# Two chained normalised 5x5 convolutions: outer output rows copied straight from PSUM, part of a row transform moved from VectorE to ScalarE and adding transfers, reflections on GpSimd, one buffer for statistics pieces

## The chip, the cores and the metric

The kernel runs on one core of one Trainium2 chip. A core has TensorE (PE, matrix products into PSUM), VectorE (DVE), ScalarE (ACT), GpSimd (POOL), SyncE (SP, which here only sends transfers) and 16 DMA engines that all queues share. The metric is device time in microseconds, lower is better. Before the change the median of three runs is 1880.79 us (1878.82 to 1884.2).

## The reference

The input x is 8 images of 32 channels, 252 x 252, float32. Two layers of the same form follow one another:

```python
def conv(x, weight):                       # 5x5, reflected edges, by FFT
    p = weight.shape[-1] // 2
    xp = jnp.pad(x, ((0, 0), (0, 0), (p, p), (p, p)), mode='reflect')
    wp = jnp.roll(zeros_like_xp.at[:, :, :5, :5].set(weight), shift=(-5 // 2, -5 // 2), axis=(-2, -1))
    out = ifft2(einsum('bihw,oihw->bohw', fft2(xp), fft2(wp))).real
    return out[:, :, p:-p, p:-p]

def _gn(v, G=16, eps=1e-5): ...            # group norm over 2 channels and all pixels

x = x + conv(_gn(x), L0_conv_weight)
x = x + conv(_gn(x), L1_conv_weight)
return x
```

So per image and layer: mean and variance of 16 groups, a 5x5 convolution of 32 to 32 channels on the normalised image, and the image itself added.

## The kernel before

**Layout.** The four pixel phases (even or odd row, even or odd column) times 32 channels lie on the 128 partitions (`quad`), so the 5x5 convolution becomes a 3x3 one of 128 to 128 channels on a quarter of the pixels. The normalisation's scale and the residual are folded into the weights of each image, and its mean goes in as a bias of one product.

**Chunks.** An image's layer is 8 chunks of 16 phase rows (`NCH`, `ROWS`), and `order` lists all chunks of all images and layers: while layer 1 of image b + 1 runs, its chunks alternate with those of layer 2 of image b. A "pair" below is a chunk of layer 2 and the layer-1 chunk beside it, some 27 us. In the code layers count from 0, so `l == 1` is layer 2. Layer 1's output stays on the chip in tiles `y`, one for a chunk, which are layer 2's input.

**Row transform.** In each group of four rows six combinations of input rows ("points" 0 to 5) are made, each is convolved along the columns with its own weights, and the six results are combined into four output rows. `transform` makes the points. It builds v (sums or differences of rows two apart) and u (two combinations, 4 times one row plus or minus the row two below), and from them `t`: point 2 (L592) is a difference of u's two halves, point 1 (L602) their sum, points 4, 3 and 0/5 (L596, L599, L609) come from v. For most chunks of layer 2 (`sent`) v is made by GpSimd's transfers: a copy of `y` into v (L557), and, once it has landed, two adding transfers (L559, L560), the second for the last two rows, which come from the next chunk's `y`. u is made by VectorE (L576, L577, and L584 for the last row). v has one buffer (tag `va`) through most of the run, so the next copy waits for L609, the last reader.

**Products.** `conv` runs on TensorE: points 2 and 4 into the banks `m`, 1 and 3 into `pairs`, on top of m's values that ScalarE puts there as a start (`seed`, L729 and L731), then 0 and 5 into `sums`. For part of the chunks (`by_columns`) points 0 and 5 use a column transform of their own (`columns`, L618 to L628, `column_product` at L707, `column_parts`), which has fewer products and more VectorE work. VectorE combines the results: L748 for differences, `inner` (L757, L758) writes output rows 1 and 2 of each group into `y`, `parts05` and `column_parts` add what rows 0 and 3 need into `sums`. ScalarE then copies rows 0 and 3 from `sums` into `y` (`outer_columns` L785, `outer` L773).

**Statistics of layer 1's input.** Each image is read a second time in 14 pieces (`load_piece` L254, tile `st`, two buffers in `spool`), and ScalarE sums each piece and its squares (L235, L241) an image ahead. `keep` does the squares for layer 2's statistics (L860) and reflects the edges of `y` by four narrow copies on ScalarE (L869 to L872).

**Output.** `store` puts layer 2's rows, of which the two column phases lie on different partitions, side by side into a tile `o` (four pairs of ScalarE copies per chunk, L925) and SP sends them out (`send_rows` L910). For the last chunk but one (`end`) VectorE and GpSimd do this.

**Order.** The order of instructions on each engine is written out by hand: `at(t, fn)` enters a step with a planned time, the table is sorted by it, and each engine runs its instructions in that order. The planned times set the order only; what is waited for follows from the data. `begin(i)` is the planned start of the i-th chunk.

Of the kernel before, what the change touches and what calls it, by code (L numbers as in the profile page):

```python
# [45 lines left out]
ALU = mybir.AluOpType  # L46
# [10 lines left out]
def tile_conv_preact_x2(ctx: ExitStack, tc: tile.TileContext, x: bass.AP, w0: bass.AP, w1: bass.AP, out: bass.AP):  # L57
# [18 lines left out]
    spool = ctx.enter_context(tc.tile_pool(name="spool", bufs=2))  # L76
# [168 lines left out]
    def load_piece(b: int, i: int):  # L245
        src = x[b].rearrange("ch h w -> (ch h w)").rearrange("(p n) -> p n", p=P)
        if b == 0:
            t = ypool.tile([P, PIECE], F32, tag="y", name=f"st_{b}_{i}")
        else:
            t = spool.tile([P, PIECE], F32, tag="st", name=f"st_{b}_{i}")  # L250
        parts = 3 if (b, i) == (0, NPIECE - 1) else 1
        m = PIECE // parts
        for j in range(parts):
            S.dma_start(t[:, j * m : (j + 1) * m], src[:, i * PIECE + j * m : i * PIECE + (j + 1) * m])  # L254
        pieces[b, i] = t
# [281 lines left out]
    def transform(t0: float, t1: float, b: int, l: int, c: int, free: float = -100.0, now=(0, 0, 0)):  # L537
# [3 lines left out]
        sent = l == 1 and (b, c) != (0, 0)  # L541

# [6 lines left out]
        def row_sums(add: bool):  # L549

            t, nxt = source()
            if not add:

                i = max(order.index((b, l, c)) - order.index((B - 2, 1, NCH - 2)), 0)
                got["v"] = vpool.tile([P, ROWS, wi], F32, tag=("va", "v")[i % 2], name=f"v_{b}_{l}_{c}")
                got["vt"] = got["v"].rearrange("p (t i) w -> p t i w", i=4)
                G.dma_start(got["v"], t)  # L557
            else:
                G.dma_start(got["v"][:, 0 : ROWS - 2], t[:, 2:ROWS], accum_op=ALU.add)  # L559
                G.dma_start(got["v"][:, ROWS - 2 : ROWS], nxt[:, 0:2], accum_op=ALU.add)  # L560

# [50 lines left out]
        def columns():  # L612
# [7 lines left out]
            if m == mo:  # L620
                f = "p t e (m a) -> p (t e) a m"
                V.tensor_sub(
                    d.rearrange("p t e a m -> p (t e) a m"),
                    t[:, :, :, 0 : 2 * m].rearrange(f, a=2), t[:, :, :, 2 : 2 * m + 2].rearrange(f, a=2),
                )
            else:
                V.tensor_sub(d[:, :, :, 0], t[:, :, :, 0 : 2 * m : 2], t[:, :, :, 2 : 2 * m + 1 : 2])
                V.tensor_sub(d[:, :, :, 1, 0:mo], odd[:, :, :, 0:mo], t[:, :, :, 3 : 2 * mo + 2 : 2])  # L628
# [15 lines left out]
        else:  # L644
            if sent:
                two = begin(order.index((b, l, c)) - 2)
                at(two + 1.45, row_sums, False)
                at(two + 8.4, row_sums, True)
            else:
                at(t0, row_pairs)  # L650
            for dt, fn in ((2, row_quads), (3.2, last_rows), (3.6, point2)):
                at(t0 + dt, fn)
# [8 lines left out]
    def conv(b: int, l: int, c: int, t0: float, t1: float, t2: float = 0.0, j0: int = 0, j1: int = NT, m05=None, later: float = 10.2):  # L661
# [28 lines left out]
        def half(tile_, i: int, e: slice, m: int):  # L690

            return tile_[:, e, i * nt * ne : i * nt * ne + nt * m].rearrange("p e (t w) -> p e t w", t=nt)
# [72 lines left out]

        def outer(e: int):
# [20 lines left out]
        def column_parts():  # L787
# [5 lines left out]
            V.tensor_sub(odd, m2[:, :, :, 0:no], odd)  # L793
            V.tensor_sub(half(sums05, 1, both, no), odd, m12[:, :, :, 0:no])  # L794
# [21 lines left out]
        if columns:  # L816
# [6 lines left out]
            for i in range(2):  # L823
                at(t2 + 0.05, outer_columns, i)
# [6 lines left out]
        else:  # L831
            at(t1 + 1.5, parts05)
            at(t2 + 0.05, outer, 0)
            at(t2 + 0.05, outer, 1)
# [4 lines left out]
        else:  # L839
            store(t1 + 1.5 if m05 else t2 + 0.7, b, c, got)  # L840


    def keep(t1: float, t2, b: int, c: int, got):
# [18 lines left out]
        def reflect():  # L862
            lo, hi = (1 if c == 0 else 0), (ROWS - 1 if c == NCH - 1 else ROWS)
            y, copy, r = got["y"], A.copy, slice(lo, hi)
# [49 lines left out]
    def store(t0: float, b: int, c: int, got):  # L914

        end = (b, c) == (B - 1, NCH - 2)
        copy = V.tensor_copy if end else A.copy

        def interleave(h: int, s: int):
            if s == 0:  # L920
                pool, tag = (spool, "st") if end else (opool, "o")
                got["o", h] = pool.tile([P, 4, 2 * WOUT[1]], F32, tag=tag, name=f"o_{b}_{c}_{h}")
            r, m = 8 * h + 4 * s, (3 if (c, h, s) == (NCH - 1, 1, 1) else 4)
            for cp in range(2):
                copy(got["o", h][halves[s], 0:m, cp::2], got["y"][halves[cp], r : r + m, :])  # L925

        def send(h: int):
            got["o"] = got.pop(("o", h))
            for s in range(2):
                send_rows(b, c, h, s, got, (G, G) if end else (S, S))  # L930

        for i, t in enumerate((0, 3.3, 5.8, 7.8)):
            at(t0 + t, interleave, i // 2, i % 2)
        at(t0 + 4.6, send, 0)
        at(t0 + 9.1, send, 1)


    def store_half(t0: float, b: int, c: int, h: int, got):
        def interleave(s: int, rows: slice, engines):
            if (s, rows.start) == (0, 1):  # L940
                got["o"] = opool.tile([P, 4, 2 * WOUT[1]], F32, tag="o", name=f"o_{b}_{c}_{h}")
            for cp in range(2):
                dst, src = got["o"][halves[s], rows, cp::2], got["y"][halves[cp], 4 * s : 4 * s + 4][:, rows]
# [92 lines left out]
    for i, (b, l, c) in enumerate(order):  # L1036
# [36 lines left out]
        if l == 0 and b + 1 < B:  # L1073
            wide = 1 if b == 0 else 2
            if c == 0:
                for j in range(2):
                    at(begin(i - 1) + 1.0 if b > 1 else t0 + (8.0 if b else 1.0), load_piece, b + 1, j)
            if c < NPIECE // 2:
                for j in range(2):
# [5 lines left out]
                    if p + 2 < NPIECE:  # L1085
                        at(t + 2.6, load_piece, b + 1, p + 2)
# [50 lines left out]
```

## Time and profile before

| | before |
|---|---|
| median of three runs | 1880.79 us |
| profiled execution | 1879.27 us |
| its span | 1877.5 us |
| mean granted TensorE clock | 0.994 |
| bytes read from HBM / written | 167.15 MB / 67.39 MB |
| mean rate of the DMA engines | 197 GB/s |
| median from issue to landing: 129.0 KB added into v | 8.5 us |
| pieces `st`, 567.0 KB | 6.1 us |

The profile is of one execution; instructions are listed as start, length, engine, line and operation, with output <- input and their shapes, and in brackets the idle time before them and what ended it. Shares of the DMA engines are means over the 16. A wait for a transfer ends when the whole of it has landed. The DMA packets of `q0` are those that GpSimd sends, those of `q1` SP's.

### The profile page before, as it was taken

Reading aid. Unit: us, or ns where it says so; the run is one execution under the profiler, and the core shown is the slowest. Engines: PE = TensorE matmul, PEld = TensorE weight load, DVE = VectorE, ACT = ScalarE, POOL = GpSimd, SP = SyncE. Lnnn points to the kernel's source line nnn. Section 1 sums busy time; section 2 is a strip of 40 time slices with the busy share of each in tenths; the row PEclk is TensorE's granted clock in tenths of the full one; section 3 lists DMA queues with packets and bytes.
Section 4 is the critical chain, followed back from the end, with each engine's and each line's share of the span. In section 5 each row is a group of like instructions: output and inputs, shape, how many; then the busy total and the mean of one; then the engine's idle time right before and its main releaser. Section 6 shows DMA issues by size and latency. Waiting matters only on the chain.

```text
span 1877.5 us, 20381 instructions
## 1 busy us (share of the span) xinstructions
PE 1839.2 (98%) x5194; PEld 966.0 (51%) x5194; DVE 1731.2 (92%) x3030; ACT 1493.8 (80%) x2781; POOL 396.2 (21%) x855
## 2 busy tenths in 40 slices
PE   5999999999999999999999999999999999999998
PEld 4444455545555555555555455554555555555455
DVE  7988799999999999999999899999999999997796
ACT  5886788878887888888898798987898876765575
POOL 4543111131112211122111311113111141110211
PEclk8999999999999999999999999999999999999999
DMA  9877578878888877987878967888878866775785
GB/s 275 203 179 180 151 209 199 210 194 202 217 202 219 194 209 192 221 223 173 220 193 206 235 175 205 205 204 204 212 202 198 214 165 140 179 174 148 195 212 125
DMA packets 207110, 369.07 MB, mean 197 GB/s; under 512 B 19088, under 2 KB 173968, under 8 KB 196752
## 3 DMA queue, kind: packets, MB, share of 16 engines
q1 hardware_dynamic: 178832, 230.73, 49.8%
q0 software_dynamic: 27600, 134.20, 29.3%
q10 hardware_dynamic: 560, 2.83, 0.4%
q8 instruction: 41, 0.67, 0.2%
q14 instruction: 77, 0.63, 0.1%
HBM read 167.15 MB, written 67.39 MB: 125 GB/s over the span
## 4 chain that ended last, share of the span: by engine, by line
PE 80%; DVE 7%; DMA 6%; ACT 3%; issue 3%; SPq 0%; POOL 0%; DVEq 0%; ACTq 0%; POOLq 0%
PE m L685 28%; PE pairs L685 28%; PE sums L707 7%; PE extra L707 6%; PE sums L685 6%; PE extra L685 4%; DMA v<-y 2%; DMA st<-in_x_dram 1%; DMA v<-ytail 1%; DMA xs<-in_x_dram 1%; ACT o L925 1%; DVE sd L748 1%; DVE t L609 1%; DMA wraw<-in_L_conv_weight_dram 1%; DMA out_dram<-o 0%
## 5 line engine op out<-in xcount | busy, mean ns | idle before, releaser
L685 PE MATMUL pairs<-t,u 128*128 128x504 f32 (+2 forms) x1548 | 692.9, 586 | 5.4 <-ACT pairs L729 3.3
L685 PE MATMUL m<-t,u 128*128 128x508 f32 (+3 forms) x1560 | 674.8, 581 | 3.4 <-DVE u L526 1.9
L685 PEld LDWEIGHTS m<-t,u 128*128 128x128 f32 x1560 | 294.2, 189 | 317.1 <-issue 297.0
L685 PEld LDWEIGHTS pairs<-t,u 128*128 128x128 f32 x1548 | 290.2, 189 | 320.1 <-issue 289.1
L925 ACT COPY o<-y 64x508 f32<-64x508 f32 x496 | 327.5, 660 | 8.6
L748 DVE SCALAR_TENSOR_TENSOR sd<-sd,pairs 128x504 f32<-128x504 f32 (+2 forms) x258 | 164.2, 671 | 19.5 <-PE pairs L685 15.2
L707 PEld LDWEIGHTS extra<-sdiff,wc 128*128 128x128 f32 x680 | 125.9, 189 | 98.1 <-issue 47.8
L707 PE MATMUL extra<-sdiff,wc 128*128 128x252 f32 (+3 forms) x680 | 173.0, 376 | 3.4 <-ACT extra L711 2.3
L860 ACT ACTIVATE junk<-y,negk 128x1008 bf16<-128x1008 f32 (+1 forms) x144 | 147.4, 1024 | 31.1 <-PE extra L707 14.5
L557 POOL DMA_DIRECT2D v<-y x63 | 35.7, 567 | 622.7 <-DVE t L609 608.4
L737 ACT COPY sd<-m 128x504 f32<-128x504 f32 (+2 forms) x258 | 136.9, 581 | 33.3 <-DVE sums L794 28.1
L609 DVE SCALAR_TENSOR_TENSOR t<-v 128x1024 f32<-128x1024 f32 (+1 forms) x128 | 157.7, 1232 | 5.4 <-PE sums L685 5.4
L707 PE MATMUL sums<-d,u 128*128 128x252 f32 (+3 forms) x680 | 157.4, 374 | 0.0
L707 PEld LDWEIGHTS sums<-d,u 128*128 128x128 f32 x680 | 127.6, 189 | 24.9 <-issue 9.0
L685 PE MATMUL sums<-t,u 128*128 128x508 f32 (+5 forms) x312 | 133.6, 577 | 0.0
L567 DVE TENSOR_TENSOR v<-xs 128x1792 f32<-128x1792 f32 (+1 forms) x65 | 130.2, 2003 | 1.2
L241 ACT ACTIVATE st<-st,negk 128x1134 f32<-128x1134 f32 x98 | 121.7, 1242 | 3.2
L559 POOL DMA_DIRECT2D v<-y x63 | 54.3, 862 | 329.1 <-DMA v<-y 329.1
L159 ACT COPY xs<-xs 64x1792 f32<-64x1792 f32 (+2 forms) x97 | 109.3, 1129 | 13.4 <-POOL xs L151 11.1
L729 ACT ACTIVATE pairs<-m,means 128x504 f32<-128x504 f32 (+1 forms) x129 | 84.2, 653 | 44.5 <-PE m L685 36.0
L785 ACT ACTIVATE y<-sums 128x504 f32<-128x504 f32 (+1 forms) x158 | 94.5, 634 | 28.3 <-PE sums L707 19.2
L235 ACT ACTIVATE st<-st 128x1134 f32<-128x1134 f32 x98 | 112.5, 1148 | 5.0 <-DMA st<-in_x_dram 3.2
(174 smaller groups left out, 2529.7 us busy)
## 6 DMA issues: line engine op xcount, KB each, us to landing
v<-y POOLq DMA_DIRECT2D x63, 1032.0 KB, 6.1
st<-in_x_dram SPq DMA_DIRECT2D x111, 567.0 KB, 6.1
out_dram<-o SPq DMA_DIRECT2D x480, 126.0 KB, 5.9
v<-y POOLq DMA_DIRECT2D x63, 903.0 KB, 7.7
xs<-in_x_dram SPq DMA_DIRECT2D x96, 441.0 KB, 8.4
xs<-in_x_dram SPq DMA_DIRECT2D x44, 504.0 KB, 12.0
u<-ud SPq DMA_DIRECT2D x15, 1152.0 KB, 6.0
xs<-in_x_dram SPq DMA_DIRECT2D x16, 472.5 KB, 9.3
```

The lines of the kernel that those rows point to most:

```text
L159: copy(t[64:128, :, 0:256:2], t[0:64, :, 1:256:2])
L235: A.activation(junk, src, AF.Identity, accum_out=acc[:, 0, i : i + 1])
L241: A.activation(junk, src, AF.Square, bias=negk, accum_out=acc[:, 1, i : i + 1])
L567: (V.tensor_add if l else V.tensor_sub)(v[:, r0:r1], t[:, r0 + 2 : r1 + 2], t[:, r0:r1])
L609: stt(t, got["vt"][:, :, 0:2], 4.0 if l else -4.0, got["vt"][:, :, 2:4], ALU.mult, ALU.add)
L685: T.matmul(dst, u[:, k, 2 - i, :], rhs[:, j0 + i0 : j0 + i1, i : i + wo], start=(i == 0 and not add), stop=(i == 2), skip_group_check=add,)
L707: T.matmul(dst[:, 0, use], w, rhs[:, use], start=(i == 2), stop=True, skip_group_check=(i != 2))
L737: A.copy(got["sd"][:, 1 + e], m24[e][:, 0:n])
L748: stt(d, d, -2.0, pairs13[e][:, 0:n], ALU.mult, ALU.add)
L785: A.activation(y, src, AF.Copy, scale=1.0 - 2 * i, **total(3 * i))
L860: A.activation(dst, src, AF.Square, bias=negk, scale=1.0 if i else -1.0, accum_out=acc[:, 1, at_ : at_ + 1])
L925: copy(got["o", h][halves[s], 0:m, cp::2], got["y"][halves[cp], r : r + m, :])
```

## The change

In short:

- In `transform`, the layer-2 chunks that come directly after a layer-1 chunk (`sent_u`) no longer make u on VectorE. ScalarE writes 4 times two of every four rows into a tile `ua` (`four_times`), and GpSimd adds the other rows with three adding transfers (`outer_rows`). The steps `row_quads` and `last_rows` are left out there.
- In `conv`, layer 2's chunks whose rows 0 and 3 come late are copied from `sums` straight into an output tile (`outer_out`), no longer through `y`. The signs of the odd columns are turned in `columns` and `column_parts` for layer 2, so that a plain copy does.
- `store` sends a chunk as outer rows (0 and 3) and inner rows (1 and 2), no longer as an upper and a lower half; a transfer now writes every eighth image row, four to a channel as before. For the last chunk but one the output tiles come from `xpool`.
- The reflecting copies of `keep` go to GpSimd except in an image's first and last chunk.
- `spool` has one buffer. Pieces are loaded one ahead, no longer two; for the second image every other piece lies in `va`, which is not yet used then.

```diff
-    spool = ctx.enter_context(tc.tile_pool(name="spool", bufs=2))
+    spool = ctx.enter_context(tc.tile_pool(name="spool", bufs=1))
...
-            t = spool.tile([P, PIECE], F32, tag="st", name=f"st_{b}_{i}")
+            pool, tag = (vpool, "va") if b == 1 and i % 2 else (spool, "st")
+            t = pool.tile([P, PIECE], F32, tag=tag, name=f"st_{b}_{i}")
...
         sent = l == 1 and (b, c) != (0, 0)
+        sent_u = sent and order[order.index((b, l, c)) - 1][1] == 0
...
+        def four_times():
+
+            got["u"] = vpool.tile([P, 2, NT, wi], F32, tag="ua", name=f"ua_{b}_{l}_{c}")
+            src = source()[0].rearrange("p (t i) w -> p i t w", i=4)
+            A.activation(got["u"], src[:, 1:3], AF.Copy, scale=4.0)
+
+        def outer_rows():
+            t, nxt = source()
+            u1, u2 = got["u"][:, 0], got["u"][:, 1]
+            G.dma_start(u1, t[:, 3:ROWS:4], accum_op=ALU.add)
+            G.dma_start(u2[:, 0 : NT - 1], t[:, 4:ROWS:4], accum_op=ALU.add)
+            G.dma_start(u2[:, NT - 1], nxt[:, 0], accum_op=ALU.add)
...
-                V.tensor_sub(d[:, :, :, 1, 0:mo], odd[:, :, :, 0:mo], t[:, :, :, 3 : 2 * mo + 2 : 2])
+                V.tensor_sub(d[:, :, :, 1, 0:mo], t[:, :, :, 3 : 2 * mo + 2 : 2], odd[:, :, :, 0:mo])
...
                 at(two + 1.45, row_sums, False)
                 at(two + 8.4, row_sums, True)
+                if sent_u:
+                    at(two + 5.3, four_times)
+                    at(two + 8.5, outer_rows)
...
-            for dt, fn in ((2, row_quads), (3.2, last_rows), (3.6, point2)):
-                at(t0 + dt, fn)
+            for dt, fn in ((2, row_quads), (3.2, last_rows)):
+                if not sent_u:
+                    at(t0 + dt, fn)
+            at(t0 + 3.6, point2)
...
+        def outer_out(e: int, engines):
+
+            if e == 0:
+                got["outer"] = out_tile(b, c, "outer")
+            t = slice(*tiles(5 * e))
+            for cp, eng in enumerate(engines):
+                to, bank = got["outer"][halves[e]], sums05[halves[cp], e]
+                if columns:
+                    dst = to.rearrange("p t (j i a) -> p t i j a", i=2, a=2)[:, t, :, :, cp]
+                    src = bank[:, 0 : 2 * nt * ne].rearrange("p (i t j) -> p t i j", i=2, t=nt)[:, t]
+                else:
+                    dst, src = to[:, t, cp : 2 * wo : 2], rows(bank[:, 0:n])[:, t]
+                (eng.copy if eng is A else eng.tensor_copy)(dst, src)
...
-            V.tensor_sub(odd, m2[:, :, :, 0:no], odd)
-            V.tensor_sub(half(sums05, 1, both, no), odd, m12[:, :, :, 0:no])
+            if l:
+                V.tensor_sub(odd, odd, m2[:, :, :, 0:no])
+                V.tensor_add(half(sums05, 1, both, no), odd, m12[:, :, :, 0:no])
+            else:
+                V.tensor_sub(odd, m2[:, :, :, 0:no], odd)
+                V.tensor_sub(half(sums05, 1, both, no), odd, m12[:, :, :, 0:no])
...
-                at(t2 + 0.05, outer_columns, i)
+                if l == 0:
+                    at(t2 + 0.05, outer_columns, i)
+                else:
+                    at(t2 + 0.05, outer_out, i, (A, A))
...
-            at(t2 + 0.05, outer, 0)
-            at(t2 + 0.05, outer, 1)
+            for e in range(2):
+                if l == 0:
+                    at(t2 + 0.05, outer, e)
+                else:
+                    at(t2 + 0.05, outer_out, e, (V, V) if e and (b, c) == (B - 1, NCH - 2) else (A, A))
...
-            store(t1 + 1.5 if m05 else t2 + 0.7, b, c, got)
+            store(t1, t1 + 1.5 if m05 else t2 + 0.7, b, c, got, m05 is not None)
...
-            y, copy, r = got["y"], A.copy, slice(lo, hi)
+            y, copy, r = got["y"], A.copy if c in (0, NCH - 1) else G.tensor_copy, slice(lo, hi)
...
+    def out_tile(b: int, c: int, name: str):
+
+        pool, tag = (xpool, "xs") if last_but_one(b, c) else (opool, "o")
+        return pool.tile([P, NT, 2 * WOUT[1] + 2], F32, tag=tag, name=f"o_{name}_{b}_{c}")
+
+    def store(t1: float, t0: float, b: int, c: int, got, from_y: bool):
...
+        def interleave(name: str, k: int):
+            if k == 0:
+                got[name] = out_tile(b, c, name)
+            i = 3 * k if name == "outer" else 1 + k
+            n = NT - 1 if (c, i) == (NCH - 1, 3) else NT
+            copy = V.tensor_copy if end else A.copy
             for cp in range(2):
+                copy(got[name][halves[k], 0:n, cp : 2 * WOUT[1] : 2], got["y"][halves[cp], i : 4 * n : 4, :])
...
+        if from_y:
+            for k, t in enumerate((0, 3.3)):
+                at(t0 + t, interleave, "outer", k)
+        for k, t in enumerate((t1 + 7.0, t1 + 7.2) if end else (t0 + 5.8, t0 + 7.8) if from_y else (t1 + 8.0, t0 + 3.3)):
+            at(t, interleave, "inner", k)
+        at(t0 + (4.6 if from_y else 2.6), send, "outer")
+        at(t1 + 7.3 if end else t0 + 9.1, send, "inner")
...
-                for j in range(2):
-                    at(begin(i - 1) + 1.0 if b > 1 else t0 + (8.0 if b else 1.0), load_piece, b + 1, j)
+                for j in range(1 if b else 2):
+                    at(begin(i - 1) + 4.0 if b > 1 else t0 + (8.0 if b else 1.0), load_piece, b + 1, j)
...
-                    if p + 2 < NPIECE:
-                        at(t + 2.6, load_piece, b + 1, p + 2)
+                    ahead = 1 if b else 2
+                    if p + ahead < NPIECE:
+                        at(t + 2.6, load_piece, b + 1, p + ahead)
```

## The prediction

> **What bounds the kernel now.** I read the page first, then the table of stretches, then who waited for whom, then two pairs of chunks in the order of time. The page:
>
> ```profile
> span 1877.5 us, 20381 instructions
> PE 1839.2 (98%) x5194; PEld 966.0 (51%) x5194; DVE 1731.2 (92%) x3030; ACT 1493.8 (80%) x2781; POOL 396.2 (21%) x855
> ...
> DMA  9877578878888877987878967888878866775785
> ...
> q1 hardware_dynamic: 178832, 230.73, 49.8%
> q0 software_dynamic: 27600, 134.20, 29.3%
> ```
>
> TensorE (PE) is busy for all but 38 us of the span. A stretch in the middle, and the last one (busy us of PE, PE's weight loads, VectorE, ScalarE, GpSimd; then granted clock, share of the DMA engines, GB/s):
>
> ```profile
> 300.00:1700.00 1400.00, 1396.63 (x3937) 733.44 (x3936) 1335.75 (x2296) 1159.15 (x2164) 265.30 (x575) 1.00 0.81 199
> ```
> ```profile
> 700.00:750.00 50.00, 50.00 (x149) 27.84 (x148) 49.41 (x83) 45.07 (x81) 5.83 (x15) 1.00 0.80 190
> ...
> 1850.00:1878.00 28.00, 18.13 (x75) 13.33 (x73) 11.93 (x32) 13.02 (x29) 4.60 (x8) 0.88 0.46 108
> ```
>
> From 300 to 1700 PE lacks 3.4 us of 1400 at clock 1.00. Its idle time is the first 36 us (20 us), 9 us in holes up to 1850 and 10 us in the tail. The change leaves every matmul as it is, so it can win only from some 9 + 10 us; the head is not touched. VectorE (DVE) is full too (49.4 of 50), yet freeing it moves the end only where PE waits for it. What can move the end is a new wait. The waits that the change leans on:
>
> ```profile
> POOL v L557 <- DVE t L609: 608.4, 52, 23.9
> POOL v L559 <- DMA v<-y: 329.1, 61, 9.1
> ...
> DVE t L596 <- DMA v<-y: 17.6, 7, 3.5
> ```
>
> GpSimd (POOL) waits for L609, which frees the buffer v, sends the copy, waits until it has landed, and only then sends the two additions. They have slack at L596 except in seven pairs. One pair of chunks where they land in time:
>
> ```profile
> 693.18 0.55 POOL L557 DMA_DIRECT2D v<-y  x1 [13.08 <-DVE t L609]
> ...
> 700.27 0.86 POOL L559 DMA_DIRECT2D v<-y  x1 [6.02 <-DMA v<-y]
> ...
> 700.81 1.21 POOL L560 DMA_DIRECT2D v<-y  x1
> ...
> 713.82 0.70 DVE L592 TENSOR_TENSOR t<-u 128x516 f32<-128x516 f32 x1
> ```
>
> and one where they don't:
>
> ```profile
> 766.15 0.70 DVE L592 TENSOR_TENSOR t<-u 128x516 f32<-128x516 f32 x1
> 766.76 0.75 DVE L602 SCALAR_TENSOR_TENSOR t<-u,means 128x516 f32<-128x516 f32 x1
> 770.43 0.70 DVE L596 SCALAR_TENSOR_TENSOR t<-v 128x516 f32<-128x516 f32 x1 [2.91 <-DMA v<-y]
> ```
>
> L592 reads u, which VectorE makes itself now. After the change u is finished by transfers that POOL sends behind L560.
>
> **Part 1, row combinations.** They move for the layer-2 chunks that follow a layer-1 chunk: 64 less all 8 of the last image, (0,0), (0,1) and (6,7), so 53. VectorE loses L576, L577 and L584: 0.70 + 0.56 + 0.29 = 1.55 us each, 82 us in all. At the end that is worth nothing, since PE fills the time; without PE as the bound it would be 82 us. ScalarE (ACT) gets one operation of 1032 columns; by L235 (1134 columns, 1.15 us) 1.05 us. POOL issues three more transfers, 0.57 to 1.2 us each by L557 and L560, so 1.7 to 3.6 us; behind them stand the border copies of xs (next at 707.93, waiting for a load until then), so that costs nothing; without that wait, up to 3.6 us of later loads' edges.
>
> The transfers: 4 + 3 + 1 rows of 516 bytes on 128 partitions, 1024 rows, 516 KB. No row of the page shows such packets. From below by bytes: q0 moved 134.2 MB in 29.3% of 1877.5 us, 244 KB/us, so 2.2 us of all 16 engines. From above by packets: q1's 178832 took 49.8%, 84 ns each, so 1024 x 84 / 16 = 5.4 us. Between them by the trace's records of single adding packets: 104 ns at 1032 bytes, 565 ns at 7224 (medians), a straight line gives 66 ns at 516, so 4.2 us, which I take, as it is the same kind of packet. Over 53 chunks that is 223 us (117 to 286). From 300 to 1700 the DMA share goes from 0.81 to 0.97 (0.89 to 1.01): nearly no idle left.
>
> When do they land? They queue behind L560's, whose median from issue to landing is 8.5 us: 700.81 + 8.5 = 709.3. ScalarE's input is there by then. With 4.2 us alone: 713.5. With the xs loads of q1 (1008 KB, some 4.8 us of 16 engines, issued 700.8 to 703.8), one packet against one, 709.3 + 4.2 + 4.8 = 718.3. Nearer to the first, because POOL's row stores are recorded in packets of 3 to 5 rows, so one of q1's single rows goes between several of q0's; I take 4.2 x 1.25, so 714.6, 0.7 us after L592's time of 713.82 (0 to 4.5). Queued behind L592 on VectorE are L602, L596, both L748 and what follows to L609, 7.3 us without a gap, and L609's end releases the next L557. That loop has no slack, so the lateness goes into each pair's period although VectorE has 1.55 us less to do. L592 starts 20.6 us (or more) after L557 in 34 of the 53 pairs: 34 x 0.7 = 24 us (0 to 153).
>
> In 19 pairs it starts after only 16 to 18 us, like 766.15 above, behind loads of four quadrants. There the additions already land at 770.4; u lands at 774.6, and L592 and L602, which lay in the wait's shadow, follow: L596 starts at 770.43 + 4.2 + 1.35 = 776.0, 5.6 us late. PE needs t24 at 773.76 and would get it at 775.3, 1.6 us late. Between 1.6 (the rest is caught up) and 5.6 (all of it goes round the loop) I take 3.6: 19 x 3.6 = 68 us (30 to 106).
>
> The Trainium skill has a rule that bears on this (DMA: Bandwidth & Descriptors, "Anatomy of one DMA — SWDGE (gpsimd) path"): such a transfer costs a fixed 2.0 us and its bytes at 436 GB/s. L560's 129 KB would be 2.3 us by that; the row has 8.5. By the page the three would add an estimated 1.2 us, land in time in the 34 pairs, and cost 19 x 1.3 = 24 us, so 1904 us. The same page ("Issuing engines are not separate DMA queues") speaks against the change: transfers of all issuers share the same 16 engines.
>
> **Part 2, outer rows from PSUM.** For layer-2 chunks with late outer rows ScalarE did two L785 (1.13 us) and four L925 (2.66); now four copies of 64 partitions out of PSUM, by L744 (0.57 from PSUM) to L925 (0.66) 2.3 to 2.6 us. It saves 1.2 to 1.5 us, about what Part 1 adds: zero at the end, since ScalarE has 10% idle. sums05 is freed at about the same point, as 2.3 us stand where L785 and two L925 took 2.5.
>
> **Part 3, reflections.** 4 x 0.22 us leave ScalarE for 48 chunks. POOL's small copies take 0.2 to 0.5 us; it is 21% busy, and an image passes before layer 2 reads these edges. Zero; if they delayed L557 or L559, up to 2 us a pair.
>
> **Part 4, one statistics buffer.** Each piece is now loaded between two neighbouring uses. Packet records show that in 20 of the 42 pairs that load pieces the load sent at that point now lands 0.7 to 2.9 us, mean 1.75, after the next L235 starts (for 713.40: last packet 715.58, L235 at 714.64); its piece has a second buffer today. With 0.7 us from last packet to release that is 2.45 us late, and ScalarE's margin before the seed L729 is needed by PE (722.75 against 721.47) is 1.3. So 20 x 1.15 = 23 us by itself; but it falls at the same moment as the wait at L592, and I add nothing while that one is as long.
>
> **Part 5, the tail.** Copies move ahead; 0 to 1 us won.
>
> **Sum.** 1879.3 (the profiled execution: span and 1.8 us around it, 1.5 us under the shown median) + 24 + 68 = 1971 us.
>
> **Rivals.** *The statistics buffer decides* (chance 0.25): with 4.2 us of new transfers ahead of the piece, ScalarE is 6.65 late, 5.35 past its margin, in 20 pairs: 107 us in place of 20 x 0.7 there, so 1971 - 14 + 107 = 2064. For it: the order of SP's queue, xs loads ahead of pieces. Against: the 0.9 us of reflections gone just before it, and a longer period leaves the DMA engines time. *No change* (0.12): the rows ride in the DMA engines' idle time, L592 finds u ready, PE stays the bound: 1878, within 3. For it: share 0.81 and PE at 99.8%. Against: the 19 pairs. It decides if u lands within 16 us of L557, and pieces in 10 us. *Faster* (0.06): VectorE's 1.55 us fill PE's holes and the tail shortens, 5 of the 9 us and 3 of the 10: 1871. Against: most holes stand behind ScalarE. That only 53 of 64 chunks change and VectorE's relief buys nothing is part of the second.
>
> **How the numbers follow.** The forecast has 0.57. A measurement here tells 0.3% (5.6 us) from no change. Faster 0.06, same 0.11, slower 0.83. Low end 1880, which leaves out the faster case and half of no change; high end 2065, the first rival. It also agrees with the engines' limit: a demand of 0.97 of 1400 us, 1358 us, filled to 0.9 would take 1509 us, 109 more.
>
> **What would show it.** Right: a wait of L592 for a transfer into u, some 0.5 to 3 us in the 34 pairs and over 4 us in the others; DMA share 0.9 in the middle; PE idle 90 us more. Waits of L235 for st, 3 us and more, mean the first rival. L592 without waits, or landings of the new rows under 6 us, make the prediction wrong.

## The result, and the profile after

The change makes the kernel **slower by 11.9%**: 2104.77 us against 1879.8 in the same comparison (four executions each), ratio 1.1193 with a 95% interval of 1.1161 to 1.1224. Its profiled execution took 2104.84 us, the span is 225.6 us longer. The forecast was 1971 us, range 1880 to 2065: the sign held, the size did not. One execution further down, of two_buffers_u_vector, was disturbed (1987 us) and is left out of that kernel's ratio.

The code has moved: the products L685 and L707 of before are now L705 and L727, the load L254 of a piece is L255, `inner` (L757) is L777; L592, L602, L596 and L609 are L607, L617, L611 and L624; L557, L559 and L560 are L559, L561 and L562; L729 is L749, L785 is L819, L792 is L826, L860 is L904, L910 is L986, L925 is L978. New are L568 (`four_times`), L573 to L575 (`outer_rows`), L798 (`outer_out`) and L913 to L916 (the reflections).

The head of the page of after, and two of its queues:

```profile
span 2103.1 us, 20506 instructions
PE 1901.7 (90%) x5194; PEld 974.3 (46%) x5194; DVE 1659.1 (79%) x2869; ACT 1496.8 (71%) x2522; POOL 646.0 (31%) x1206
...
q1 hardware_dynamic: 178832, 230.73, 42.8%
q0 software_dynamic: 84416, 162.21, 38.0%
```

VectorE lost 72 us of work (82 forecast), ScalarE's stayed, GpSimd's grew by 250 us. TensorE ran the same 5194 matmuls and stood still far more: summing its idle times of over 0.15 us after the first 50 us gives 174.6 us against 8.8 before, and 134.2 of that stand directly before products into `pairs`, which start from ScalarE's seed (L749). It was also 62.5 us longer busy with the same matmuls. Who waited for whom:

```profile
DVE sums L826 <- ACT o_outer L798: 168.2, 40, 11.2
...
ACT st L235 <- DMA st<-in_x_dram: 145.1, 29, 16.1
PE pairs L705 <- ACT pairs L749: 129.5, 44, 10.8
DVE t L607 <- DMA ua<-y: 113.3, 28, 10.7
...
DVE t L607 <- DMA ua<-ytail: 45.5, 6, 8.5
```

Three new waits stand beside one another, one for each large part: VectorE for the copies out of `sums` (L798), ScalarE for a statistics piece (L235), VectorE for the transferred u (L607). The forecast had only the third in its sum. The waits can't be added: they fall into the same moments. One such moment, on SP's queue and ScalarE (start, length, and in brackets the idle time before):

```profile
841.17 7.66 SPq L143 DMA_DIRECT2D xs<-in_x_dram  x6
848.88 11.35 SPq L143 DMA_DIRECT2D xtail<-in_x_dram  x8
860.27 1.88 SPq L986 DMA_DIRECT2D out_dram<-o_inner  x4
862.25 0.41 SPq L255 DMA_DIRECT2D st<-in_x_dram  x1
```
```profile
867.11 1.15 ACT L235 ACTIVATE st<-st 128x1134 f32<-128x1134 f32 x1 [13.75 <-DMA st<-in_x_dram]
...
870.74 2.44 ACT L798 COPY o_outer<-sums 64x508 f32<-64x508 f32 x4
873.20 0.66 ACT L749 ACTIVATE pairs<-m,means 128x508 f32<-128x508 f32 x1
```

The piece leaves SP behind fourteen loads and four stores. ScalarE stands 13.75 us for it; behind L235 are queued the copies that free `sums` and the seed. TensorE in the order of time, and all engines in stretches of 5 us (busy us of PE, weight loads, VectorE, ScalarE, GpSimd; granted clock; DMA share; GB/s):

```profile
873.91 5.06 PE L705 MATMUL pairs<-t,u 128*128 128x508 f32 x8 [8.47 <-ACT pairs L749]
...
889.03 3.54 PE L705 MATMUL pairs<-t,u 128*128 128x504 f32 x8
```
```profile
865.00:870.00 5.00, 0.44 (x2) 0.00 (x0) 0.00 (x0) 2.86 (x5) 0.45 (x2) 0.99 0.64 248
870.00:875.00 5.00, 1.09 (x2) 0.58 (x3) 1.76 (x3) 4.92 (x9) 1.61 (x2) 0.50 0.89 206
875.00:880.00 5.00, 5.00 (x13) 2.56 (x12) 5.00 (x7) 3.45 (x7) 1.92 (x3) 0.83 0.98 226
880.00:885.00 5.00, 5.00 (x19) 3.40 (x18) 4.89 (x11) 4.86 (x10) 1.57 (x2) 1.00 1.11 139
```

After 8.47 us of idleness eight matmuls take 5.06 us instead of 3.54. The granted clock stands at 0.50; in stretches of half a microsecond it is 0.50 up to 876.5, 0.75 up to 877 and 1.00 from there on, so it is full again some 3 us after the first matmul. So a long wait is paid a second time (mean clock 0.967, before 0.994). In the whole trace PE is busy for 89.7 us at a granted clock of 0.50, against 6.8 before. Half of the difference, an estimate of 41 us, is what the clock adds to PE's busy time; where the other 21 of the 62.5 us come from is not shown. In changed_8byte_ahead below PE is 34 us longer busy than before at a mean clock of 0.991, so it is not the clock alone. The Trainium skill says that gaps of more than about 3 us between bursts of matmuls drop the clock to half (TensorE: Matmul & The Clock Gate, "Why this matters for your kernels"); this row agrees.

### The profile page after: what moved, and what is told of

Same layout as the page of the kernel before. It is cut to its first block, busy times and chain, and to the rows that moved or that the text cites. A ratio compares the mean times of both kernels' runs of the same rounds, so it can differ in the third digit from the quotient of the medians.

```text
span 2103.1 us, 20506 instructions
## 1 busy us (share of the span) xinstructions
PE 1901.7 (90%) x5194; PEld 974.3 (46%) x5194; DVE 1659.1 (79%) x2869; ACT 1496.8 (71%) x2522; POOL 646.0 (31%) x1206
## 4 chain that ended last, share of the span: by engine, by line
DMA 27%; PE 21%; DVE 15%; issue 14%; ACT 10%; SPq 5%; POOL 4%; ACTq 0%; DVEq 0%; POOLq 0%
PE pairs L705 9%; DMA st<-in_x_dram 7%; PE m L705 6%; DMA v<-y 5%; DMA xs<-in_x_dram 5%; DMA ua<-y 5%; ACT o_outer L798 4%; DMA ua<-ytail 4%; SPq L143 3%; PE extra L705 2%; DMA out_dram<-o_inner 2%; SPq L986 2%; PE sums L705 2%; ACT junk L904 2%; ACT st L235 1%
## 5 line engine op out<-in xcount | busy, mean ns | idle before, releaser
L705 PE MATMUL pairs<-t,u 128*128 128x504 f32 (+2 forms) x1548 | 736.6, 616 | 134.8 <-ACT pairs L749 129.5
L705 PE MATMUL m<-t,u 128*128 128x508 f32 (+3 forms) x1560 | 677.3, 583 | 6.1 <-DVE t L607 2.9
L705 PEld LDWEIGHTS pairs<-t,u 128*128 128x128 f32 x1548 | 301.1, 199 | 490.8 <-issue 307.6
L705 PEld LDWEIGHTS m<-t,u 128*128 128x128 f32 x1560 | 294.0, 190 | 323.8 <-issue 295.7
L798 ACT COPY o_outer<-sums 64x512 f32<-64x512 f32 (+1 forms) x242 | 215.2, 889 | 59.8 <-DMA out_dram<-o_inner 23.5
L235 ACT ACTIVATE st<-st 128x1134 f32<-128x1134 f32 x98 | 112.5, 1148 | 145.6 <-DMA st<-in_x_dram 145.1
L559 POOL DMA_DIRECT2D v<-y x63 | 36.6, 581 | 580.1 <-DVE t L624 564.1
L727 PE MATMUL extra<-sdiff,wc 128*128 128x252 f32 (+3 forms) x680 | 174.6, 378 | 28.1 <-DVE sdiff L634 16.7
L826 DVE TENSOR_TENSOR sums<-extra,sd 128x512 f32<-128x512 f32 (+1 forms) x85 | 58.9, 693 | 169.4 <-ACT o_outer L798 168.2
L727 PEld LDWEIGHTS extra<-sdiff,wc 128*128 128x128 f32 x680 | 124.6, 189 | 129.8 <-issue 53.7
L757 ACT COPY sd<-m 128x504 f32<-128x504 f32 (+2 forms) x258 | 136.9, 581 | 63.3 <-DVE sums L829 43.2
L978 ACT COPY o_inner<-y 64x508 f32<-64x508 f32 x248 | 163.7, 660 | 4.2 <-DMA out_dram<-o_outer 2.2
L904 ACT ACTIVATE junk<-y,negk 128x1008 bf16<-128x1008 f32 (+1 forms) x144 | 147.6, 1026 | 25.1 <-PE extra L727 14.6
L607 DVE TENSOR_TENSOR t<-ua 128x516 f32<-128x516 f32 x53 | 36.8, 694 | 160.7 <-DMA ua<-y 113.3
L624 DVE SCALAR_TENSOR_TENSOR t<-v 128x1024 f32<-128x1024 f32 (+1 forms) x128 | 158.4, 1238 | 4.2 <-PE sums L705 4.2
L727 PE MATMUL sums<-d,u 128*128 128x252 f32 (+3 forms) x680 | 157.3, 373 | 0.0
L561 POOL DMA_DIRECT2D v<-y x63 | 53.6, 851 | 320.5 <-DMA v<-y 315.1
L727 PEld LDWEIGHTS sums<-d,u 128*128 128x128 f32 x680 | 127.4, 189 | 25.1 <-issue 7.1
L148 POOL COPY xs<-xs 64x4 f32<-64x4 f32 (+3 forms) x113 | 51.0, 451 | 279.3 <-DMA xs<-in_x_dram 271.3
L749 ACT ACTIVATE pairs<-m,means 128x504 f32<-128x504 f32 (+1 forms) x129 | 84.3, 653 | 69.8 <-PE m L705 53.1
L705 PE MATMUL sums<-t,u 128*128 128x508 f32 (+5 forms) x312 | 133.2, 575 | 0.0
```

Source lines behind the costliest of these rows:

```text
L235: A.activation(junk, src, AF.Identity, accum_out=acc[:, 0, i : i + 1])
L624: stt(t, got["vt"][:, :, 0:2], 4.0 if l else -4.0, got["vt"][:, :, 2:4], ALU.mult, ALU.add)
L705: T.matmul(dst, u[:, k, 2 - i, :], rhs[:, j0 + i0 : j0 + i1, i : i + wo], start=(i == 0 and not add), stop=(i == 2), skip_group_check=add,)
L727: T.matmul(dst[:, 0, use], w, rhs[:, use], start=(i == 2), stop=True, skip_group_check=(i != 2))
L749: A.activation(dst, src, AF.Identity, bias=norm[b, l][1][:, 0:1])
L757: A.copy(got["sd"][:, 1 + e], m24[e][:, 0:n])
```

## The experiments

"Against before" is the ratio to the kernel before in the same comparison, with its 95% interval. Times of parts are differences of these ratios times 1880 us, or of the medians. Diffs are against the changed kernel, where nothing else is said.

**The parts taken back, one after another.** First u on VectorE again, the rest as changed.

```diff
-        sent_u = sent and order[order.index((b, l, c)) - 1][1] == 0
+        sent_u = False
```

> The changed kernel with u made by VectorE again in all chunks (no ScalarE start, no adding transfers into ua); the rest of the change stays. Theory 1 (late rows of u decide): L607 waits no more (it waited some 160 us in the changed kernel), DMA share falls to about 0.77, and the time falls by 120 us or more, to 1980 or below. Theory 2 (ScalarE decides: the column chunks' outer copies at 1.07 us each and the wait for st lie in front of the seed of pairs): PE's waits for the seed (about 130 us) stay, and the time falls by 80 us at most, to 2020 or above.

Measured: 2025.7 us, 1.0784 [1.0753, 1.0816] against before. Moving u costs 77 us of the changed kernel's 224; 147 us are left without it, with the waits of L235 (109.3 us) and of L826 for L798 (148.9 us). So in this order the transfers are a third of the loss. They weigh more in another order, as will be seen.

Next, two statistics buffers again as well (all pieces in `spool`, and the first loads at their places of before):

```diff
+        sent_u = False
...
-    spool = ctx.enter_context(tc.tile_pool(name="spool", bufs=1))
+    spool = ctx.enter_context(tc.tile_pool(name="spool", bufs=2))
...
-                    ahead = 1 if b else 2
+                    ahead = 2
```

> The changed kernel with u made by VectorE and two buffers for the statistics pieces again (loads two ahead): what is left of the change is the outer rows out of PSUM (16-byte steps) and the reflections on GpSimd. If late pieces and late rows of u are all of the loss, 1875 to 1890. If the outer copies of 4.3 us cost by themselves, 1900 to 1950, with PE waiting for the seed of pairs.

Measured: 1.0425 [1.0402, 1.0448] against before, some 1959 us. Then rows 0 and 3 through `y` again too, so that only the new order of sending and the reflections on GpSimd are left of the change (with the sign of the copies in L819 and the flag of `store` to match):

```diff
-                if l == 0:
+                if l == 0 or not last_but_one(b, c):
                     at(t2 + 0.05, outer_columns, i)
...
-                if l == 0:
+                if l == 0 or not last_but_one(b, c):
                     at(t2 + 0.05, outer, e)
```

> The kernel of two_buffers_u_vector (fast runs near 1958) with rows 0 and 3 through y: what is left of the change is the split of a chunk into outer and inner rows when it is sent and the reflections on GpSimd. If the copies out of PSUM are all that is left of the loss, 1876 to 1886; if the new order of sending costs, 1890 or more.

Measured: 1877.06 us (ten executions), 0.9982 [0.9971, 0.9992]: at the time of before, at most 0.3% under it. It is the fastest version of this study, too close to before to be called a gain. The stretch in the middle, columns as above, has PE at 1196.5 of 1200 us, as before:

```profile
300.00:1500.00 1200.00, 1196.52 (x3377) 627.74 (x3375) 1144.58 (x1971) 997.23 (x1769) 267.45 (x622) 1.00 0.83 205
```

The four ratios make one chain (times 1880 us):

| kernel | against before | the step adds |
|---|---|---|
| sending order and reflections alone | 0.9982 | -3 us |
| + rows 0 and 3 straight from PSUM | 1.0425 | 83 us |
| + one statistics buffer | 1.0784 | 67 us |
| + u by ScalarE and transfers (the changed kernel) | 1.1193 | 77 us |

**The statistics buffer alone**, put into the kernel before, with the change's places for the pieces of the second image, its places for the first loads, and `xpool` for the output tiles of the last chunk but one (diff against before):

```diff
-    spool = ctx.enter_context(tc.tile_pool(name="spool", bufs=2))
+    spool = ctx.enter_context(tc.tile_pool(name="spool", bufs=1))
...
-                    if p + 2 < NPIECE:
-                        at(t + 2.6, load_piece, b + 1, p + 2)
+                    ahead = 1 if b else 2
+                    if p + ahead < NPIECE:
+                        at(t + 2.6, load_piece, b + 1, p + ahead)
```

> The kernel before with only the single buffer for statistics pieces (loads one ahead). By the prediction's term it costs 23 us, so about 1903, and L235 waits for st in some 20 pairs. If the buffer is the larger share of the loss, 1940 or more. If it costs only in company of the new transfers, 1880 to 1890.

Measured: 1959.76 us, 1.0433 [1.0403, 1.0464]: 81 us by itself. Its waits, and one of them on ScalarE:

```profile
ACT st L235 <- DMA st<-in_x_dram: 123.1, 24, 16.3
```
```profile
576.13 1.15 ACT L235 ACTIVATE st<-st 128x1134 f32<-128x1134 f32 x1 [14.98 <-DMA st<-in_x_dram]
```

Six waits of 12.2 to 16.3 us, each in another image, make 84.7 us of it. The kernel before shows where they come from, on SP's queue and on ScalarE:

```profile
533.59 14.49 SPq L143 DMA_DIRECT2D xtail<-in_x_dram  x8
548.18 1.80 SPq L910 DMA_DIRECT2D out_dram<-o  x4
550.09 0.87 SPq L254 DMA_DIRECT2D st<-in_x_dram  x2
```
```profile
541.63 1.14 ACT L235 ACTIVATE st<-st 128x1134 f32<-128x1134 f32 x1
...
559.28 1.15 ACT L235 ACTIVATE st<-st 128x1134 f32<-128x1134 f32 x1
```

With two buffers the load of 550.09 has until 559.28. With one, the first load at this place of the queue is the one that the use of 541.63 needs, and it is not even sent by then: with a landing of 6 to 7 us it is some 15 us late. If that is the cause, sending the piece ahead of the loads of x must remove it. In the one-buffer version of before:

```diff
-                        at(t + 2.6, load_piece, b + 1, p + ahead)
+                        at(t + 0.05, load_piece, b + 1, p + ahead)
...
-                        at(t0 + 9.5, load, kb, kc, *part)
+                        at(t0 + 9.9, load, kb, kc, *part)
```

> The kernel before with one statistics buffer, as before_one_buffer, but SP sends a piece's load as soon as the piece before it is summed, ahead of the loads of xs and xtail. If the 80 us of one buffer come from the place in SP's queue, L235's waits fall from 123 us to under 40 and the time to 1880 to 1900. If they come from the transfer itself (6 us from issue to landing) or from holding up xs, it stays at 1930 or more.

Measured: 1903.17 us, 1.0122 [1.0103, 1.0141]. 58 of the 81 us are gone, and the waits of L235 fall from 123.1 to 17.0 us:

```profile
ACT st L235 <- DMA st<-in_x_dram: 17.0, 9, 5.6
```

So most of the buffer's price is a place in a queue. 23 us are left, which no run here takes apart.

**The copies out of PSUM.** In after, ScalarE's groups by form (count, busy us, mean ns, idle time before them):

```profile
L798 ACT COPY o_outer<-sums 64x512 f32<-64x512 f32 x140 | 149.9, 1071 | 26.7 <-DMA out_dram<-o_inner 15.1 <-PE sums L727 7.7 <-issue 2.3
L798 ACT COPY o_outer<-sums 64x508 f32<-64x508 f32 x88 | 54.0, 613 | 32.8 <-PE sums L705 23.4 <-DMA out_dram<-o_inner 8.4
```

The first form, of the chunks by columns, writes one number every 16 bytes and takes 1071 ns; the second writes every 8 bytes and takes 613. Turning the order of the inner loops gives the first form steps of 8 bytes too:

```diff
-                    dst = to.rearrange("p t (j i a) -> p t i j a", i=2, a=2)[:, t, :, :, cp]
-                    src = bank[:, 0 : 2 * nt * ne].rearrange("p (i t j) -> p t i j", i=2, t=nt)[:, t]
+                    dst = to.rearrange("p t (j i a) -> p t j i a", i=2, a=2)[:, t, :, :, cp]
+                    src = bank[:, 0 : 2 * nt * ne].rearrange("p (i t j) -> p t j i", i=2, t=nt)[:, t]
```

> The changed kernel with one edit: the column chunks' copy out of PSUM writes its 512 columns in the order of the output row, 8 bytes from one to the next, and jumps between the two halves in PSUM; before it wrote 16 bytes from one to the next and read in order. If the step of 16 bytes makes the copy slow, it takes 0.6 us in place of 1.07 and the time falls by 50 us or more, to 2050 or below (theory 2). If the two-dimensional pattern or the half partitions make it slow, it stays at 1.0 us or more and the time at 2105.

```profile
L798 ACT COPY o_outer<-sums 64x512 f32<-64x512 f32 x140 | 85.9, 613 | 20.6 <-PE sums L727 13.1 <-DMA out_dram<-o_inner 3.6 <-issue 2.3
```

The copies take 613 ns, 64 us of ScalarE's work are gone, and the time is the same: 2101.79 us, 1.119 [1.1113, 1.1266]. ScalarE now waits at L235 for 176.9 us instead of 145.1; the piece comes when it comes. The Trainium skill says that SBUF lies in lines of 16 bytes and that at least two accesses must hit a line to hide the latency of an access (Advanced Engine Details and Errata, "Memory Cachelines"); the step of the output here, 8 against 16 bytes, agrees. Where neither the single buffer nor the new u stands in the way, the same edit must pay:

> The kernel of two_buffers_u_vector with the column chunks' copies in 8-byte steps (0.61 us in place of 1.07). Expected 1870 to 1885 if the two large parts are those undone here; the difference to two_buffers_u_vector is the price of the 16-byte steps: 2 us a pair at most, 0 to 60 us.

Measured: 1918.32 us, 1.0213 [1.0192, 1.0234], 40 us less than with steps of 16 bytes. So of the 83 us about half is the step. In what is left, VectorE waits for the copies, and the copies for an output tile; the same moment on SP's queue, ScalarE and VectorE:

```profile
ACT o_outer L798 <- DMA out_dram<-o_inner: 57.8, 9, 7.3
...
DVE sums L826 <- ACT o_outer L798: 51.1, 12, 6.9
```
```profile
543.28 10.30 SPq L143 DMA_DIRECT2D xtail<-in_x_dram  x8
553.62 1.87 SPq L986 DMA_DIRECT2D out_dram<-o_inner  x4
```
```profile
557.78 2.47 ACT L798 COPY o_outer<-sums 64x508 f32<-64x508 f32 x4 [6.76 <-DMA out_dram<-o_inner]
```
```profile
560.28 0.69 DVE L826 TENSOR_TENSOR sums<-extra,sd 128x504 f32<-128x504 f32 x1 [6.33 <-ACT o_outer L798]
```

Seven times, an image apart, ScalarE stands 6.6 to 7.3 us for a tile whose stores SP sends behind fourteen loads, and VectorE waits 4.6 to 6.9 us for ScalarE, 43 of its 51.1 us. Before, the two L785 freed `sums` after 1.12 us and needed no output tile; now it takes four copies of 64 partitions, 2.4 us with steps of 8 bytes and 4.25 with 16, and they need the tile first. The seed stands behind them.

**All mends together, with and without the new u.** The changed kernel with steps of 8 bytes and pieces sent ahead:

> The whole change, with the copies in 8-byte steps and the pieces' loads ahead of xs in SP's queue. If three separate causes add up (pieces 80 us, 16-byte steps some 50, rows of u some 80), it comes to 1960 to 1990, and VectorE's waits for ua are the largest left. If the DMA engines' load is the real bound, it stays at 2060 or more whatever the order.

Measured: 2054.53 us, 1.0923 [1.0896, 1.0951], far over the 1960 to 1990 that three separate causes would have left: the causes do not add up. Against outer_8byte_steps, sending the pieces ahead saves 47 us here. The waits for `st` and `o_outer` are nearly gone (10.3 and 7.2 us), and u's has grown from 113.3 to

```profile
DVE t L607 <- DMA ua<-y: 215.2, 43, 10.6
```

The same with u on VectorE (`sent_u = False`):

> The kernel of changed_8byte_ahead (2055) with u made by VectorE: no start on ScalarE and no transfers into ua. The difference of the two is the price of moving u. If late rows of u and the DMA engines' load hold the pair, about 1930 (1920 to 1950), 105 to 135 us less; if other waits take their place, 1980 or more.

Measured: 1913.11 us, 1.0181 [1.0165, 1.0196]. With the other waits mostly out of the way the new u costs 141 us, not 77. A third output tile there (`opool` with `bufs=3`):

> The kernel of u_vector_8byte_ahead with three output tiles in place of two. In two_buffers_u_vector_8byte the copies out of PSUM waited 58 us for an output tile that was still being sent. If that wait is what is left of the loss, it goes and the time falls by 20 to 40 us, to 1880 to 1910. If not, it stays within 10 us of u_vector_8byte_ahead.

1911.91 us, 1.0175 [1.0157, 1.0193]: no difference, so in this kernel the output tile is not what is left. It does not settle two_buffers_u_vector_8byte: with the loads of x moved back, SP sends the inner rows ahead of them, and ScalarE waits for an output tile only once here (4.1 us), VectorE for the copies 8.2 us in all. 34 us over before are left, of which one buffer with the same order of loads costs 23 without this part (before_one_buffer_ahead).

**Load or lateness of the new rows.** In the mended kernel, the transfers stay, but nobody reads their result, and VectorE makes u:

```diff
-            got["u"] = vpool.tile([P, 2, NT, wi], F32, tag="ua", name=f"ua_{b}_{l}_{c}")
+            got["ua"] = vpool.tile([P, 2, NT, wi], F32, tag="ua", name=f"ua_{b}_{l}_{c}")
...
-                if not sent_u:
-                    at(t0 + dt, fn)
+                at(t0 + dt, fn)
```

> The kernel of u_vector_8byte_ahead (1913: VectorE makes u) to which ScalarE's start and the three adding transfers into ua come back, but nobody reads ua. What it adds over 1913 is load alone (DMA engines, GpSimd's queue, ScalarE's 1.07 us), without a wait for late rows. If the load is the cause of the 141 us that the move of u costs, 2020 to 2060. If lateness is, 1915 to 1950.

Measured: 1945.79 us, 1.0354 [1.0335, 1.0373]. Against u_vector_8byte_ahead, where VectorE does the same work, the load alone costs 33 of the 141 us; the DMA share from 300 to 1500 is 0.91 instead of 0.83. The other 109 come with reading the result, although VectorE then has 1.55 us less to do per chunk. Two ways to wait less were tried. Points 2 and 1, which read u, and point 4 with them, later in VectorE's order:

```diff
-            at(t0 + 3.6, point2)
+            after_inner = free + (11.06 if by_columns(*now) else 10.21)
+            at(after_inner if sent_u else t0 + 3.6, point2)
...
-            at(max(t0 + 5.5, free + 7.8), point1)
+            at(after_inner + 0.01 if sent_u else max(t0 + 5.5, free + 7.8), point1)
```

> The kernel of changed_8byte_ahead (2055) with the points made from u (and point 4) put some 3 us later in VectorE's order, behind inner. If what costs is that VectorE stands at u with other work behind it, some 2 us a pair are won: 1930 to 1980. If the chain from the release of v through the transfers back to it is the bound, later points lengthen it or leave it: 2045 or more.

Measured: 2022.37 us, 1.0764 [1.0734, 1.0794], 32 us won. TensorE then waits for L607 itself, which comes late now: 59.1 us in place of 36.6. And the rows sent earlier, ahead of the additions into v:

```diff
-                    at(two + 5.3, four_times)
-                    at(two + 8.5, outer_rows)
+                    at(two - 3.3, four_times)
+                    at(two - 0.5, outer_rows)
```

> The kernel of changed_8byte_ahead (2055) with ScalarE's start and the three transfers into ua sent before GpSimd waits for the release of v, some 10 us sooner, so that they no longer stand behind the two additions into v. If the place in GpSimd's queue makes u late and that is the cost, L607's waits for ua (272 us) fall under 60 and the time to 1890 to 1930. If the DMA engines' load is, the additions into v come late in their place: 2000 or more, with waits at L611.

Measured: 1970.81 us, 1.0505 [1.0471, 1.0539], 84 us won. L607 no longer waits; in its place

```profile
DVE t L611 <- DMA v<-y: 144.7, 31, 7.8
```

and the first addition into v lands after 10.4 us instead of 7.9 (medians). The transfers that are sent first delay the others: the wait is passed on, in part, and does not vanish.

**Two more.** Reflections on ScalarE again, in the version two_buffers_u_vector_8byte:

```diff
-            y, copy, r = got["y"], A.copy if c in (0, NCH - 1) else G.tensor_copy, slice(lo, hi)
+            y, copy, r = got["y"], A.copy, slice(lo, hi)
```

> The kernel of two_buffers_u_vector_8byte (1918) with the reflections on ScalarE again. By the prediction the place of the reflections costs nothing: 1910 to 1925. If GpSimd's copies or what they hold up matter, 1895 or less.

1923.40 us, 1.0229 [1.0207, 1.0251], against 1.0213: GpSimd's reflections cost nothing that can be told from noise. And rows 0 and 3 through `y` in the otherwise complete changed kernel (the diff is that of two_buffers_outer_through_y):

> The changed kernel with rows 0 and 3 of layer 2 copied into y and interleaved from there, as before the change (last chunk but one left as changed); transfers into ua, one statistics buffer and GpSimd reflections stay. Theory 2: ScalarE's work in front of the seed falls from 4.3 to about 2.5 us, PE's waits for the seed from 130 to under 80 us, time 2000 to 2050. Theory 1: time within 30 us of 2105, because the pair goes on waiting for u.

Measured: 2333.89 us, 1.2425 [1.2389, 1.2461], so 229 us more than the changed kernel. VectorE's `inner` waits:

```profile
DVE y L777 <- DMA ua<-y: 444.0, 39, 17.8
```

The tile that `inner` writes is one which the transfers just sent still read. A layer-2 tile of `y` is then held until its rows 0 and 3 are copied; that this is why another buffer comes up was not tried by itself. The row shows VectorE standing for the transfers that read `y`, of which there are nine tiles, and the two times that the parts of the change lean on each other: without the new u, and with two statistics buffers, the same edit saves 83 us.

## Why the prediction was right or wrong

**Which step failed.** Two terms that the forecast set to zero. They are 150 of the 224 us in the chain of ratios, more than the 134 that were missed. How the loss divides depends on the order, as the waits hide one another: with steps of 8 bytes and pieces ahead first, these take off some 50 us, u then 140, and 34 are left. By that order the third term, Part 1's 92 us, was too small as well.

**Part 4, one statistics buffer** ("20 x 1.15 = 23 us by itself; ... I add nothing"). It costs 81 us by itself and 67 on top of the PSUM copies. The forecast compared each load with the use of L235 that came next after it was sent. In one pair of each image SP is so late that the use which the load would serve with one buffer has already gone by: the load of 550.09 had to be held against 541.63, not 559.28, and is 15 us late. These six long waits were not seen. That 23 us are left once the piece is sent ahead (1.0122) is the forecast's number by luck: L235 then waits 17.0 us in 9 cases, not in 20 pairs. Adding nothing was wrong too: with u moved as well, sending the pieces ahead still saves 47 us (2101.79 to 2054.53).

**Part 2, outer rows from PSUM** ("2.3 to 2.6 us", "sums05 is freed at about the same point"). Right for chunks by rows (2.44 us for four), wrong for those by columns (4.25), whose 16-byte step the priced rows did not have. And `sums` was not freed after two L785 and two L925 but after the two L785, 1.12 us; the kernel before shows it:

```profile
576.43 1.12 ACT L785 ACTIVATE y<-sums 128x512 f32<-128x512 f32 x2
577.59 1.35 ACT L925 COPY o<-y 64x508 f32<-64x508 f32 x2
578.96 0.66 ACT L729 ACTIVATE pairs<-m,means 128x508 f32<-128x508 f32 x1
```

"Zero at the end, since ScalarE has 10% idle" mistook an average for slack: the copies stand in front of the seed and of L826. And the sum had no term for the output tile, which these copies must now wait for before they can free `sums`. Measured, 83 us.

**Part 1, row combinations** (24 + 68 = 92 us). The mechanism was right, VectorE waits for the rows. The size was fair on top of the rest (77 us) and too small where the other waits are mostly out of the way (141), which is what the forecast priced, with the other parts at nothing. The packets were right: q0 has 56,816 more, 54,272 of them with 516 bytes and a median of 66 ns, 4.4 us of all engines per chunk against 4.2. Transfers into `ua` land after 10.3 to 12.4 us (medians). L607 waits 159 us in 34 cases, not in all 53 pairs, and for up to 10.7 us. So the waits are fewer and longer than forecast, 4.7 us in the mean. The issues on GpSimd take 1.7, 2.2 and 2.4 us in the mean (0.57 to 1.2 forecast). In unread_rows the same issues and transfers stand, and cost 33 us together.

**What would show it.** TensorE was to stand idle 90 us more; it was 166. The DMA share was to be 0.97 by the sum, 0.9 as what would show it; measured 0.84 from 300 to 1500, as the work is spread over a longer time, and 0.91 and 0.93 where the mended kernel runs faster:

```profile
300.00:1500.00 1200.00, 1079.71 (x2933) 550.67 (x2932) 942.76 (x1612) 888.59 (x1499) 370.95 (x666) 0.97 0.84 193
```

**Parts 3 and 5.** Reflections and the tail cost nothing, as forecast, and neither does the new sending order, which the sum did not price (0.9982 with all of them).

**The rivals.** The statistics buffer does decide a large part, as the first one said, but not by 5.35 us in each of 20 pairs: most of it is one long wait in each image. Its 2064 us was still too low, as Part 2 stands beside it and Part 1. *No change* and *faster* fell: with 72 us less work for VectorE the kernel is slower.

**Left open.** Some 40 us of Part 2 remain with steps of 8 bytes. The seven waits for an output tile fit, but TensorE's idle time directly behind them is 12 us; the rest would have to come from a VectorE that has no slack to catch up. How the 40 us divide between the output tile and the longer copies is not shown by an edit of its own.

## What to carry to other kernels

When a buffer is taken away, hold each load against the use that it will then serve, in the order of the queue that sends it, and look for the one period in which that queue is longest; a count of typical periods hides it. Price a copy by a row with the same step on its output, and ask what it must wait for and what is released by its end, not how much of its engine is idle. Several parts that each cost nothing on average can wait at the same moment of a full schedule, so take them back one at a time, in more than one order, before blaming the largest.

## What was unexpected of the hardware

- ScalarE's copy of 64 x 512 numbers from PSUM took 1071 ns with 16 bytes between outputs and 613 ns with 8.
- An adding transfer of GpSimd made one packet of every row (516 bytes, 66 ns median), where its row stores have 3 to 5 rows in one; issuing 512, 384 and 128 such rows took it 1.7, 2.2 and 2.4 us in the mean, so the fewest rows the longest.
- Three adding transfers sent ahead of two others raised the first one's landing from 7.9 to 10.4 us, and landed themselves in 4.9 to 6.7 us instead of 12.8 to 14.7 (medians).
- After 8.47 us without a matmul TensorE ran at a granted clock of 0.50, and at full clock only some 3 us after its first matmul.
